# Attention's edges in a four-layer image kernel: a split image load, a pair of queries moved behind a branch, a last chunk ended by products, and norms in text order

## The chip, the cores and the metric

The kernel runs on one core of a Trainium2 chip. The metric is the device time of one execution in microseconds (us). Three runs of the kernel before the change gave 7595.06, 7599.12 and 7599.31 us; the median is 7599.12 us. One further execution was taken with the hardware profiler, and all views shown are of that one. Engines are named as the profile names them: PE is TensorE, DVE is VectorE, ACT is ScalarE, POOL is GpSimd, SP is SyncE, which here only issues transfers.

## The reference

One image of 48 channels and 128 x 128 pixels, float32, passes through four layers with residuals:

```
x = x + attention(group_norm(x))      # layer 0
x = x + sweeps(group_norm(x))         # layer 1
x = x + patch_conv(group_norm(x))     # layer 2
x = x + scan(group_norm(x))           # layer 3
```

`group_norm` has 16 groups of 3 channels and takes mean and variance over a group's whole image. Layer 0 makes queries, keys and values by a 1x1 convolution and a 3x3 depthwise one, divides each query and key by its length, multiplies the scores of all 16384 pixels against all 16384 by a temperature, takes a softmax, sums the values, and applies a 48 x 48 projection. Layer 1 runs four recurrences, one row or column a step, in which a row receives a 5-tap convolution of the row before: down, up, right, left. Layer 2 is a convolution with products of 8x8 Fourier transforms, layer 3 a state-space scan. The change touches layer 0, the way into layer 1, and the loading of the image.

## The kernel before

**Storage.** Two large tiles, `xa` and `xb`, are used again and again. In attention `xa` is called `xq`, `xb` is called `other`. The image is loaded into partitions 0 to 47 of `xa`, in eight transfers on SP's queue (L1549), followed there by the sweep weights. In `xb` the columns 0 to 8191 become the keys `k` (pixels of the first half of the image on partitions 0 to 63, of the second on 64 to 127), the columns above the values `v`. The queries are written over the image in `xa`, on partitions 0 to 63 by VectorE and again on 64 to 127 by a ScalarE copy.

**Statistics and bands.** 32 `bn_stats` (L162) over 512 pixels each, then `group_stats` (L71 to L87): an aggregation, two tiny products that average over a group, a square root on ScalarE, a reciprocal. The convolution runs over eight bands of 16 rows. For a band, VectorE writes the normalised rows (L93), SP copies them to partitions 64 to 111 (L188) and parts of them to the free partitions (L190), and makes twelve small copies for the taps that are left (`rest`, L199). Two `bands` tiles alternate, and the next band is prepared while this one is worked on. A band is worked on in two pairs of 512 pixels: `conv` is the products, `take` squares, sums, takes the root (`nrm`), transposes the values (`pt`), and scales queries and keys by the reciprocal length on VectorE (L263 to L271). TensorE and ScalarE instructions are held to text order by `InOrder`; other engines are ordered by a scheduler.

**The branch.** A register is loaded from `absT`, the size of the temperature, and all engines branch: to `attend` when it is at most 32, which is the case here, else to `attend_shifted`, which subtracts each query's largest score.

**attend.** 32 chunks of 512 queries; in each 64 key tiles `j`, each with four score products (L48, `s`), one exponential of 128 x 1024 on ScalarE (`e`), and four products that add weighted values and weights into `acc`. The sums follow two tiles behind the scores (`BEHIND`). A chunk is ended by `Finish`: ScalarE copies `acc` to `o`, VectorE adds its two halves (`both`, L366), ScalarE copies the upper partitions down (`second`), VectorE adds (L372) and takes the reciprocal of the weights' sums (L375), SP copies the reciprocals to the channels' partitions in three transfers (L378), VectorE multiplies, adds the image, and takes `bn_stats` of the result (L382 to L384), and SP stores the chunk to `x1` (L385). For all chunks but the last these steps lie under the next chunk's products.

**Into layer 1.** POOL clears borders in `xb` and sets a row of ones (`borders`, L610 to L614); `group_stats` again; 32 ScalarE instructions of 8 rows (L623) write the normalised image twice into `xb`; then the sweeps start: each step has an input product (L653), three state products (L678) and a VectorE multiplication by a mask into the next row.

Of the kernel before, what the change touches and what calls it, by code (L numbers as in the profile page):

```python
# [65 lines left out]
def group_stats(nc, pool, psum, const, name="gn_ps"):  # L66


    st, gmat = const["st"], const["gmat"]
    mv = pool.tile([C, 2], F32, name="gn_mv")  # L70
    nc.vector.bn_aggr(mv, st)  # L71
    pm = psum.tile([C, 1], F32, name=name)
    nc.tensor.matmul(pm, lhsT=gmat, rhs=mv[:, 0:1], start=True, stop=True)
    mean = pool.tile([C, 1], F32, name="gn_mean")
    nc.vector.tensor_copy(mean, pm)

    dev = pool.tile([C, 1], F32, name="gn_dev")
    nc.vector.tensor_sub(dev, mv[:, 0:1], mean)
    var = pool.tile([C, 1], F32, name="gn_var")
    nc.vector.scalar_tensor_tensor(var, dev, dev, mv[:, 1:2], ALU.mult, ALU.add)  # L80
    pv = psum.tile([C, 1], F32, name=name)
    nc.tensor.matmul(pv, lhsT=gmat, rhs=var, start=True, stop=True)
    std = pool.tile([C, 1], F32, name="gn_std")
    nc.vector.tensor_scalar_add(std, pv, 1e-5)
    nc.scalar.activation(std, std, AF.Sqrt)
    rstd = pool.tile([C, 1], F32, name="gn_rstd")
# [27 lines left out]
def attention(ctx, tc, xq, other, x1, const, ins):  # L114


    nc = tc.nc
# [11 lines left out]
    nc.sync.dma_start(proj[0:GAP, 0:C], ins["l0_proj"])  # L129
    temp = kv.tile([128, 1], F32, name="temp")  # L130
    nc.sync.dma_start(temp, ins["l0_temp"].to_broadcast([128, 1]))
# [5 lines left out]
    nc.vector.tensor_mul(absT, temp, sgn)  # L137

    with ExitStack() as a:
# [21 lines left out]
        for i in range(NQ):  # L161
            nc.vector.bn_stats(st[:, i, :], xq[0:C, i * CH : (i + 1) * CH])  # L162
        stats = group_stats(nc, wp, ps2, const, name="pss")
# [9 lines left out]
        def band(b):  # L173

            t, e = bands[b % 2], rests[b % 2]
            first = b * R - 1
            lo, hi = max(first, 0), min(first + R + 2, H)
            normalise(  # L180
                nc,
                t[0:C, lo - first : hi - first, 1 : W + 1],
                rows(xq[0:C, lo * W : hi * W]),
                stats,
            )
            if b == NB - 1:
                nc.gpsimd.memset(t[0:C, hi - first : hi - first + 1, :], 0.0)
            nc.sync.dma_start(t[64 : 64 + C, 0 : R + 1], t[0:C, 1 : R + 2])  # L188
            for n in range(2):
                nc.sync.dma_start(  # L190
                    t[64 * n + C : 64 * n + 64, 0:R], t[16 * n : 16 * n + 16, 2 : R + 2]
                )

            two = t[32:C, 2:, :].rearrange("c (k n i) w -> c n k i w", n=2, i=4)
            for i in range(R // 8):
                for n in range(2):
                    for dx in range(3):
                        at = 64 * n + 16 * dx
                        nc.sync.dma_start(e[at : at + 16, i], two[:, n, i, :, dx : dx + W])  # L199
            return t, e  # L200
# [39 lines left out]
        def take(t0, p, pv):  # L240
# [8 lines left out]
            for n in range(2):  # L249
                psss.append(ps2.tile([128, CH], F32, name="pss"))  # L250
                pe.matmul(psss[n], lhsT=blk, rhs=sqs[n], start=True, stop=True)
                nrms.append(sp.tile([128, CH], F32, name="nrm"))
                act.activation(nrms[n], psss[n], AF.Sqrt)
            pt = ps1.tile([128, 4, 2, 64], F32, name="pt")
# [6 lines left out]
            left = []  # L261
            for n in range(2):
                nc.vector.tensor_scalar_max(nrms[n], nrms[n], 1e-12)  # L263
                rn = sp.tile([128, CH], F32, name="rn")
                nc.vector.reciprocal(rn, nrms[n])
                q = slice(t0 + n * CH, t0 + (n + 1) * CH)
                nc.vector.scalar_tensor_tensor(
                    xq[0:64, q], p[n][0:64], sgn[0:64], rn[0:64], ALU.mult, ALU.mult
                )
                left.append(q)  # L270
                nc.vector.tensor_mul(  # L271
                    k[kb : kb + 64, tk + n * CH : tk + (n + 1) * CH], p[n][64:128], rn[64:128]
                )
            nc.vector.tensor_copy(
# [8 lines left out]
        for b in range(NB):  # L283
            nxt = band(b + 1) if b + 1 < NB else None
            for y in range(0, R, 8):
# [4 lines left out]
                for q in left:  # L290
                    act.copy(xq[64:128, q], xq[0:64, q])
# [1455 lines left out]
```

## Time and profile before

| | |
|---|---|
| median of three runs | 7599.12 us |
| the profiled execution | 7597.49 us |
| its span, first to last instruction | 7595.7 us |
| PE busy | 6125.8 us, 81% |
| ACT busy | 4410.3 us, 58% |
| DVE busy | 3378.7 us, 44% |
| POOL busy | 2792.3 us, 37% |
| attention's score and sum products | 252.47 to about 3778 us |
| first product of the sweeps | 3804.74 us |

A line of the timeline has the start and the duration in us, the engine (with q: its queue, where transfers are issued), the line of the kernel, the operation, what is written and read, the shapes, and how many such instructions are merged in the line; in brackets stand the idle time before it and what ended it. Where an order is kept by the helper `InOrder`, the line is L48 for all instructions, so that tiles' names tell them apart. A row of the windows has, for a stretch of time, its length and then the busy time and count of PE, PE's weight loads, DVE, ACT and POOL, then the granted TensorE clock, the mean busy share of the 16 DMA engines, and GB/s. The chain is the work that ended last, followed back from the last instruction.

### The profile page before, as it was taken

What the parts mean: (1) busy time and instruction counts of PE and PEld (TensorE: products, weight loads), DVE (VectorE), ACT (ScalarE), POOL (GpSimd) and SP (SyncE); (2) the same over time, 40 slices, a digit from 0 to 9 for tenths busy, and PEclk for the clock granted to TensorE, in tenths of its full rate; (3) what the DMA queues carried; (4) which work ended last, traced back from release to release, by engine and by line L of the source; (5) the groups of instructions that cost most, each with busy time, mean ns of one, the idle gap of its engine ahead of it and who ended that gap; (6) DMA issues with size and microseconds to landing.
All of it is one profiled execution on the core that took longest, in us unless ns stands there. A gap on an engine that the chain in (4) does not pass through costs nothing.

```text
span 7595.7 us, 203249 instructions
## 1 busy us (share of the span) xinstructions
PE 6125.8 (81%) x93756; PEld 3162.8 (42%) x93756; DVE 3378.7 (44%) x2497; ACT 4410.3 (58%) x4868; POOL 2792.3 (37%) x574
## 2 busy tenths in 40 slices
PE   7999999999999999999988889755545545554555
PEld 3333333333333333333367755334334343343444
DVE  8300000000000000000022234499999999999998
ACT  2566666666666666666625003366666667666665
POOL 0000000000000000000000022299999999999998
PEclk9999999999999999999999999876767767776666
DMA  3000000000000000000000011166556665656775
GB/s 66 8 4 4 4 3 4 4 4 3 4 4 3 4 4 4 3 4 4 4 1 17 1 33 37 46 160 165 158 158 167 156 160 154 164 159 164 177 181 150
DMA packets 182350, 484.85 MB, mean 64 GB/s; under 512 B 35859, under 2 KB 67778, under 8 KB 179506
## 3 DMA queue, kind: packets, MB, share of 16 engines
q1 hardware_dynamic: 175471, 464.69, 24.0%
q8 instruction: 735, 12.04, 0.7%
q10 hardware_dynamic: 6019, 7.09, 0.4%
q14 instruction: 125, 1.02, 0.0%
HBM read 428.03 MB, written 22.02 MB: 59 GB/s over the span
## 4 chain that ended last, share of the span: by engine, by line
PE 58%; DVE 24%; issue 7%; POOL 4%; ACT 2%; DMA 1%; SPq 0%; DVEq 0%; POOLq 0%; ACTq 0%
PE s L48 23%; PE acc L48 23%; DVE h L1504 20%; PE p L678 6%; POOL h L1497 3%; PE y L48 2%; DVE xb L48 1%; DVE xa L48 1%; DMA du<-rep 1%; PE pp L48 1%; PE pc L48 1%; PE po L48 1%; ACT dA L48 1%; DVE y L48 0%; POOL y L901 0%
## 5 line engine op out<-in xcount | busy, mean ns | idle before, releaser
L48 ACT ACTIVATE e<-s,absT 128x1024 f32<-128x1024 f32 x2048 | 2279.2, 1115 | 1197.5 <-PE s L48 1196.7
L1497 POOL TENSOR_TENSOR h<-du,bt 128x3072 f32<-128x3072 f32 (+1 forms) x386 | 2560.0, 6672 | 83.2 <-DMA du<-rep 62.1
L48 PE MATMUL s<-xa,xb 49*64 49x512 f32 x16384 | 2133.9, 589 | 10.6 <-DVE xb L271 10.6
L48 PE MATMUL acc<-e,xb 64*64 64x512 f32 x16384 | 2131.9, 588 | 0.0
L1504 DVE TENSOR_TENSOR_SCAN h<-dA,carry,h 128x1024 f32<-128x1024 f32 x864 | 1939.8, 2329 | 43.3 <-ACT dA L48 27.2
L48 ACT ACTIVATE dA<-dt,a 128x1024 f32<-128x1024 f32 x1152 | 1287.3, 1118 | 867.5 <-DVE h L1504 856.4
L48 PE MATMUL y<-h,cw 128*32 128x48 f32 x49152 | 886.2, 244 | 933.2 <-issue 499.0
L366 DVE TENSOR_TENSOR both<-o 128x512 f32<-128x512 f32 x32 | 22.2, 693 | 3078.6 <-ACT o L48 3078.6
L614 POOL MEMSET xa<- 48x128 f32 x1 | 0.3, 326 | 3523.5 <-PE acc L48 3523.5
L48 PEld LDWEIGHTS y<-h,cw 128*32 128x32 f32 x49152 | 796.5, 138 | 1057.8 <-issue 653.1
L48 PEld LDWEIGHTS s<-xa,xb 49*64 49x64 f32 x16384 | 643.9, 132 | 1129.9 <-issue 587.3
L48 PEld LDWEIGHTS acc<-e,xb 64*64 64x64 f32 x16384 | 643.1, 132 | 1118.9 <-issue 1096.0
L1504 DVE TENSOR_TENSOR_SCAN h<-dA,h 128x1024 f32<-128x1024 f32 x288 | 633.9, 2270 | 44.8 <-ACT dA L48 36.0
L48 PE MATMUL yz<-ev,sel 128*8 128x48 f32 x4096 | 193.5, 260 | 280.0 <-ACT ev L48 274.3
L48 PEld LDWEIGHTS yz<-ev,sel 128*8 128x8 f32 x4096 | 162.7, 106 | 338.3 <-ACT ev L48 305.9
L678 PE MATMUL p<-xb,l_w 112*112 112x129 f32 x1524 | 233.6, 289 | 42.6 <-DVE xb L48 42.5
L678 PE MATMUL p<-xa,l_w 112*112 112x129 f32 x1524 | 232.2, 288 | 41.9 <-DVE xa L48 41.9
L699 POOL TENSOR_TENSOR xb<-xb,xa 48x2048 f32<-48x2048 f32 (+2 forms) x10 | 44.7, 4465 | 559.0 <-DVE xa L48 559.0
L678 PEld LDWEIGHTS p<-xb,l_w 112*112 112x112 f32 x1524 | 181.9, 177 | 94.1 <-DVE xb L48 94.1
L661 ACT COPY xa<-xb 48x128 f32<-48x128 f32 x256 | 107.3, 419 | 194.5 <-issue 136.0
L678 PEld LDWEIGHTS p<-xa,l_w 112*112 112x112 f32 x1524 | 180.6, 176 | 93.3 <-DVE xa L48 93.3
L48 PE MATMUL pc<-wt,xa 128*128 128x288 f32 x768 | 198.8, 416 | 7.4 <-DMA xa<-xa 7.4
(186 smaller groups left out, 3349.7 us busy)
## 6 DMA issues: line engine op xcount, KB each, us to landing
du<-rep SPq DMA_DIRECT2D x768, 256.0 KB
dt<-rep SPq DMA_DIRECT2D x768, 256.0 KB
rep<-dd SPq DMA_DIRECT2D x24, 192.0 KB
yd<-ys ACTq DMA_DIRECT2D x256, 12.0 KB
rest<-xa SPq DMA_DIRECT2D x90, 38.0 KB
band<-band SPq DMA_DIRECT2D x8, 414.4 KB
xa<-in_x_dram SPq DMA_DIRECT2D x8, 384.0 KB
rest<-band SPq DMA_DIRECT2D x96, 32.0 KB
```

Source lines behind the costliest of these rows:

```text
L48: ins = method(*args, **kwargs).ins
L366: nc.vector.tensor_add(self.both, o[:, 0], o[:, 1])
L614: nc.gpsimd.memset(b[64:K, lines, E + W - 1 : E + W], 0.0)
L661: nc.scalar.copy(u[at : at + C, :, y], t[0:C, E + h, E : E + W])
L678: nc.tensor.matmul(p, lhsT=w[0:K, which, i, :], rhs=state[0:K, 2 * i : 2 * i + L], start=False, stop=(i == 2),)
L699: nc.gpsimd.tensor_add(xr, xr, u[0:C, x : x + xr.shape[2], E : E + H].rearrange("c w h -> c h w"),)
L1497: nc.gpsimd.tensor_mul(h[:, p, ks], du.unsqueeze(1).to_broadcast([128, ks.stop - ks.start, LC]), r["bt"][:, ks],)
L1504: nc.vector.tensor_tensor_scan(h[:, p, k, :], dA, h[:, p, k, :], carry[:, i, k : k + 1] if ci else 0.0, ALU.mult, ALU.add,)
```

## The change

The image is loaded into `xb` instead: the first half of the pixels on partitions 0 to 47, the second on 64 to 111, in alternate transfers, with POOL memsets ahead on partitions 32 to 63. `bn_stats` covers both halves in 16 instructions, and a new table `gmat2` averages over groups and halves. The first band is prepared in two parts, of which the first one's small copies are issued on ACT's queue; the loads of `proj` and `temp` move from SP's queue to ACT's. The last pair's norms and products are copied by ScalarE to `late`, and their scaling is put into both branches (`scale`, `again`). Attention's last chunk adds partitions by two products with a 0-1 matrix (`adder`) instead of by copies; its store to `x1` is issued behind the branch. After the branch ScalarE takes a square root of `absT`, which nothing reads. The chunk pool has one buffer instead of two. The borders' memsets go by 16 rows, and the fills are in text order with two smaller ones first. The core of the diff:

```
-        for i in range(NQ):
-            nc.vector.bn_stats(st[:, i, :], xq[0:C, i * CH : (i + 1) * CH])
-        stats = group_stats(nc, wp, ps2, const, name="pss")
+        K2 = 64 + C
+        halves = wp.tile([K2, NQ // 2, 6], F32, name="halves")
+        for i in range(NQ // 2):
+            nc.vector.bn_stats(halves[:, i, :], other[0:K2, i * CH : (i + 1) * CH])
+        mean, rstd = group_stats(nc, wp, ps2, halves, const["gmat2"], name="pss")
+        stats = mean[0:C], rstd[0:C]
...
+            for p0, p1 in [(0, 10), (10, R + 2)] if b == 0 else [(0, R + 2)]:
+                for half, x in enumerate((other[0:C], other[64 : 64 + C])):
+                    lo = max(first + p0, half * H // 2)
+                    hi = min(first + p1, (half + 1) * H // 2)
+                    if lo < hi:
+                        at = half * H // 2
+                        normalise(
+                            nc,
+                            t[0:C, lo - first : hi - first, 1 : W + 1],
+                            rows(x[:, (lo - at) * W : (hi - at) * W]),
+                            stats,
+                        )
...
+                queue = nc.scalar if b == 0 and p0 == 0 else nc.sync
+                for i in range(to.start // 8, to.stop // 8):
+                    for n in range(2):
+                        for dx in range(3):
+                            at = 64 * n + 16 * dx
+                            queue.dma_start(e[at : at + 16, i], two[:, n, i, :, dx : dx + W])
...
+            if t0 == N - 2 * CH:
+                for n in range(2):
+                    act.copy(late[n], p[n])
+                p = late
...
+            def scale():
+                for n in range(2):
+                    nc.vector.tensor_scalar_max(nrms[n], nrms[n], 1e-12)
+                    rn = rnp.tile([128, CH], F32, name="rn")
+                    nc.vector.reciprocal(rn, nrms[n])
...
+            if p is not late:
+                scale()
...
+    end = slice(N - CH, N)
+    nc.sync.dma_start(x1[:, end], xq[0:C, end])
+    nc.scalar.activation(absT, absT, AF.Sqrt)
+
+def adder(nc, pool, ident):
+    add = pool.tile([128, 64 + C], F32, name="add")
+    nc.vector.memset(add, 0.0)
+    for b in (0, 64):
+        nc.vector.tensor_copy(add[b : b + C, 0:C], ident[b : b + C, b : b + C])
+        nc.vector.tensor_copy(
+            add[b + 32 : b + 64, 64:], ident[b + 32 : b + 64, b + C : b + C + 1].to_broadcast([32, C])
+        )
+    return add
...
-    sp = ctx.enter_context(tc.tile_pool(name="l0_b", bufs=2))
+    sp = ctx.enter_context(tc.tile_pool(name="l0_b", bufs=1))
...
+    def end():
+        cols = slice(N - CH, N)
+        xres = sp.tile([C, CH], F32, name="xres")
+        nc.sync.dma_start(xres, ins["x"][:, cols])
+        o = sp.tile([128, 2, CH], F32, name="o")
+        act.copy(o, acc)
+        p = ps_s.tile([128, 2, CH], F32, name="s")[0 : 64 + C, 0]
+        for part in range(2):
+            pe.matmul(p, lhsT=add, rhs=o[:, part], start=(part == 0), stop=(part == 1))
+        rec = sp.tile([64, CH], F32, name="rec")[0:C]
+        nc.vector.reciprocal(rec, p[64 : 64 + C])
+        nc.vector.tensor_mul(rec, p[0:C], rec)
+        nc.vector.tensor_add(xq[0:C, cols], rec, xres)
+        nc.vector.bn_stats(st[:, NQ - 1, :], xq[0:C, cols])
+
+    scale, again = last
+    scale()
+    add = adder(nc, ep2, ident)
...
+            if c == 0 and j == KT // 2:
+                again(act.copy)
...
-    finish = Finish(NQ - 1, acc)
-    finish.divide()
-    finish.result()
+    end()
...
-        nc.gpsimd.memset(b[32:64, lines, inside], 1.0)
+        for r in range(lines.start, lines.stop, 16):
+            some = slice(r, r + 16)
+            nc.gpsimd.memset(b[32:64, some, inside], 1.0)
+            nc.gpsimd.memset(b[0:C, some, E - 1 : E], 0.0)
...
-    RN = 8
-    for r in range(0, H, RN):
+    act = InOrder(tc, nc.scalar)
+    for lo, hi in [(0, 2), (2, 8)] + [(r, r + 8) for r in range(8, H, 8)]:
         for at, x in ((0, E), (64, E - 1)):
-            nc.scalar.activation(
+            act.activation(
...
-        for i in range(0, N, 2048):
-            nc.sync.dma_start(xa[0:C, i : i + 2048], ins["x"][:, i : i + 2048])
+        for i in range(0, N // 2, 2048):
+            nc.gpsimd.memset(xb[32:64, i : i + 2048], 0.0)
+            for half in range(2):
+                at = half * N // 2 + i
+                nc.sync.dma_start(
+                    xb[64 * half : 64 * half + C, i : i + 2048], ins["x"][:, at : at + 2048]
+                )
```

## The prediction

> **What bounds the kernel now.** I read the page first, for which work follows which, then the timeline of the four places that the change touches, then the windows of the first 30 us and the waits of SyncE. The profiled execution took 7597.49 us (span 7595.7, so 1.8 us lie around it); the median of the three runs, 7599.12, stands 1.6 us above it.
>
> ```profile
> PE 58%; DVE 24%; issue 7%; POOL 4%; ACT 2%; DMA 1%; SPq 0%; DVEq 0%; POOLq 0%; ACTq 0%
> ```
>
> The chain that ended last is mostly TensorE: attention's score and sum products, then the row-by-row sweeps, then the scan on VectorE. None of these loops is altered. What the change can win lies in the gaps between stages, where the chain passes from engine to engine. There are three.
>
> *Start.* From the timeline, the windows and SyncE's waits:
>
> ```profile
> 0.74 9.86 SPq L1549 DMA_DIRECT2D xa<-in_x_dram  x8
> 12.35 17.49 DVE L162 BATCH_NORM_STATS2 st<-xa 48x6 f32<-48x512 f32 x29
> 29.87 1.01 DVE L71 BATCH_NORM_AGGREGATE gn_mv<-st 48x2 f32<-48x192 f32 x1
> 33.18 3.92 DVE L93 TENSOR_SCALAR band<-xa,gn_mean,gn_rstd 48x2176 f32<-48x2176 f32 x2
> 35.74 0.64 SPq L188 DMA_DIRECT2D band<-band  x1
> 36.42 3.35 SPq L190 DMA_DIRECT2D band<-band  x2
> 42.46 7.86 PE L48 MATMUL p<-band,wt 128*128 128x512 f32 x12 [10.21 <-DMA band<-band]
> ```
> ```profile
> 8.00:10.00 2.00, 0.00 (x0) 0.00 (x0) 0.00 (x0) 0.00 (x0) 0.00 (x0) 1.00 1.10 396
> 14.00:16.00 2.00, 0.00 (x0) 0.00 (x0) 2.00 (x5) 0.17 (x1) 0.00 (x0) 1.00 1.08 152
> 26.00:28.00 2.00, 0.00 (x0) 0.00 (x0) 2.00 (x5) 0.00 (x0) 0.00 (x0) 1.00 0.89 274
> ```
> ```profile
> SPq L1549 <- DMA ident<-in_c_ident_dram: 4.8, 1, 4.8
> ```
>
> VectorE takes the image's statistics without a pause to 29.84 us; then group norm, the first band, its copies, and the first product at 42.46. The last column of the windows is GB/s: the image alone (48 partitions) moves at about 150 with all DMA engines busy, tables of 128 partitions at 274 to 396. The image ends at about 26 us, so loading and statistics are nearly level.
>
> *Branch.* TensorE ends the convolution's transposes, and starts scores 10.6 us later:
>
> ```profile
> 241.27 0.60 PE L48 MATMUL pt<-ident,vt 128*128 128x128 f32 x4
> 241.47 0.60 ACT L48 ACTIVATE nrm<-pss 128x512 f32<-128x512 f32 x1 [0.26 <-PE pss L48]
> 252.47 5.40 PE L48 MATMUL s<-xa,xb 49*64 49x512 f32 x24 [10.60 <-DVE xb L271]
> ```
>
> The releaser is VectorE's scaling of the last pair of queries and keys. Between these gaps TensorE is never idle: its other waits in 43 to 240 us are none.
>
> *End of attention to the first sweep step:*
>
> ```profile
> 3778.48 1.01 ACT L48 COPY o<-acc 128x1024 f32<-128x1024 f32 x1 [1.40 <-PE acc L48]
> 3779.87 13.91 POOL L610 MEMSET xb<- 32x16512 f32 x1
> 3781.62 3.34 DVE L375 RECIPROCAL rec<-y 32x512 f32<-32x512 f32 x1
> 3784.99 1.78 SPq L378 DMA_DIRECT2D recs<-rec  x3
> 3789.70 0.69 DVE L384 BATCH_NORM_STATS2 st<-xa 48x6 f32<-48x512 f32 x1
> 3792.96 1.01 DVE L71 BATCH_NORM_AGGREGATE gn_mv<-st 48x2 f32<-48x192 f32 x1 [2.58 <-issue]
> 3795.59 1.28 ACT L85 ACT_TABLE_LOAD   x1 [14.72 <-DVE gn_std L84]
> 3797.56 39.24 ACT L623 ACTIVATE xb<-xa,off,gn_rstd 48x1024 f32<-48x1024 f32 x32 [0.47 <-DVE off L619]
> 3804.74 0.74 PE L653 MATMUL p<-xb,l_wi 112*112 112x129 f32 x2 [9.41 <-ACT xb L623]
> ```
>
> Every step here waits for the one above it, the memset excepted.
>
> **The change part by part.**
>
> *Load and statistics.* Half the image goes to partitions 0 to 47, half to 64 to 111, so one statistics instruction covers both: 16 instead of 32 at 0.668 us, 10.7 us less on VectorE. But the image must have landed. It is 8 x 384 KB, 3.15 MB; at about 150 GB/s, 21 us. If the two halves ran side by side it would be 10.5 us. The Trainium skill speaks against that: "SBUF — State Buffer", section "Can I just issue two DMAs to hit both halves?", says that two DMAs at once, one at partition 0 and one at 64, gave only 6% over one, since they serialize on the same engines. By the rule 1.2 us are saved, by the hope 10.5. No row here shows alternate halves. I stand near the rule, since all eight loads stay in one queue, and take 10%, 1.9 us. Against it: the second load now waits for the identity table, as the third does above, and for a POOL memset (32x2048, 1.7 us by 13.91 us for 16512), and behind it in SP's queue wait six loads and the sweep weights. I estimate 1 us, plus 0.3 us for a 50 KB table. The image then ends 0.6 us sooner, at about 25.3; 1 us to land, four statistics of 0.668: 29.0 instead of 29.87, **0.9 us**. Ends: 1.5 us lost if nothing runs faster; 8 us won if halves run side by side, which VectorE then caps, because in the built change all 16 statistics stand behind the weight multiply that waits for both weight loads (now queued later, the first of them behind the first image load). The POOL memsets delay the bands' memsets by 7 us, to about 13.6, with the bands written at 33. Moving two small loads from SP to ACT costs nothing: they are issued while ACT is idle.
>
> *Group norm and first band.* Aggregation over 96 values instead of 192: 0.5 of 1.01. The Sqrt table loads early, because the projection's copy is no longer late: 0.2. **0.7 us.** The first part of the band has 9 rows of 17: 2.53 us (17 rows, 1x2176) becomes 1.3, **1.2 us**. The copies before the first product shrink from 414 and 2 x 130 KB to 52% of that: about 690 KB took 4.6 us, now 2.4; 0.5 is given back to six small copies that go at once on ACT's queue: **1.7 us**. On ACT six issues of 0.64 us, 3.8 us, stand before the first square, 9 us after the first product; covered. On SP, past which they are moved, part two of the band follows; it is wanted 14.8 us after the first product. Two later bands get a normalisation more (some 0.2 us each), within VectorE's idle (22.5 us before L263 over the stage). Whole start: 0.9 + 0.7 + 1.2 + 1.7 = **4.5 us**.
>
> *Branch.* ACT copies the last pair out of PSUM (2 x 0.59, by the row of vt, same shape), and VectorE's scaling moves behind the branch. In the built change the first score waits for the pair before (done at about 240) and for the second of these copies; a wait for the last pair's keys stands at the 57th key tile, 56 x 1.72 = 96 us later, for 10.3 us of VectorE work. ACT's norm ends at 242.07, the copies at 243.3; with 0.15 us, as the old hand-over took, scores start at 243.4 instead of 252.47: **9.0 us**. TensorE's branch itself was issued at 240.8 and took 95 ns, so is no cost. ACT then makes the previous pair's two copies (1.14 us, as before), ready at 244.5; its Exp table waits for the first score tile anyway, some 2.2 us after the start. The last pair's copies stand between Exps: 1.24 us against 0.6 us idle in each of 1.72 us and two tiles of lead (sums follow scores by 2): no stall, 1.2 us if that cover is gone. The x1 store is issued behind the branch, nobody waits for 250 us.
>
> *Attention's last chunk.* Removed: both (0.69), second (0.62), y (0.68), three copies through SP (3784.99 to 3788.20, 3.2 us). Added: two products with the adder, as the norm's two pss products (1.98 us). Reciprocal, multiply, add and statistics stay. 3779.5 + 2.0 + 3.35 + 0.7 + 0.7 + 0.7 with hand-overs is 3787.1 instead of 3790.39: **3.3 us**. The adder's five small VectorE instructions lie in the first chunk, hidden.
>
> *Out of the branch.* The 2.58 us "issue" before aggregation stays: it follows VectorE's own last instruction and no transfer. The table load leaves the chain: ACT does a Sqrt at once after the branch, about 3783 (its copy at 3778.5, a jump of 3.3 us as VectorE's, the load), before aggregation at 3789.7 which waits for it: **1.3 us**.
>
> *Fill.* Before, the first product waited for the sixth fill, 7.2 us after the first began. In text order it needs two of 2 rows (256 elements, about 0.4 us each by 1.15 to 1.24 for 1024): 0.85 us, **6.3 us**. The next product wants two of 6 rows, 1.75 us, under the 2.5 us which the first step takes. Later 8 rows cost 2.4 us of ACT and 10.4 us of steps. POOL's memset of 13.91 us ended at 3793.8, which would now hold the fills (from 3793.0); in eight pieces the first fill waits for the first only, and most are released within the last chunk. If that cover failed, about 1 us.
>
> Sum: 4.5 + 9.0 + 3.3 + 1.3 + 6.3 = **24.4 us**. 7597.5 - 24.4 = 7573.1 for a profiled execution, 7574.7 by the median; I say 7574.5.
>
> **The rivals.** *Halves load side by side.* For: the windows show more than double the rate on 128 partitions with the engines busy either way, so the receiving side limits; staggered engines could use both. Against: the rule. Another 7 us: 7567.
>
> *A gap stays shut.* Scores still start after the scaling (9.0 us gone, 7583.7), or memsets, mask or jump hold the sweeps (10.9 in all gone, 7585.6). For: VectorE still has to do all of it, and was 98% busy before the branch. Against: the waits above.
>
> *Slower: single buffers.* The chunk pool goes from two buffers to one. If the copy of acc, which itself releases the one acc, had to wait for its single buffer, TensorE would stall at 31 boundaries. It ends slower by over 0.2% from (24.4 + 15.2)/31 = 1.3 us each; at 2 us the time is 7637. For: acc already waits there, 16.4 us in 31 times. Against: VectorE idles 93.66 us before both, so the buffer is free long before.
>
> **How the numbers follow.** About what a measurement can tell from no change is 0.2%, 15.2 us, or 7583.9. Main case 0.68 (7570 to 7580), side by side 0.15, gap shut 0.13 (a third still beyond the bound), slower 0.04. Faster 0.68 + 0.15 + 0.05 = 0.88, same 0.08, slower 0.04. The range reaches into the side-by-side and shut cases: 7563 to 7584.
>
> **What would show it.** Right: first statistics aggregation near 29 and first convolution product near 38; scores 1.5 us after the transposes; aggregation 11.3 us after the last sums of attention (14.6 now); the first sweep product under 1 us after the first fill. Wrong: 250 GB/s or more while only the image loads; TensorE waiting for L295 before the first score; waits of TensorE at chunk boundaries.

## The result and the profile after

The changed kernel took 7579.23 us (median of nine runs, 7572.69 to 7580.31). The kernel before took 7600.40 us beside it (median of nine, 7595.06 to 7607.28). The ratio is 0.997, 95% interval 0.996 to 0.998. That is 21.2 us less, where 24.6 were forecast. A second set, on another occasion, gave 7574.90 us (five runs) against 7603.35 (nine): 0.9964, interval 0.9950 to 0.9977, 28.5 us less. The forecast of 7574.5 lies just under both medians of the changed kernel, its gain of 24.6 us between the two gains.

The profiled execution of the changed kernel took 7579.86 us (span 7578.1). First its start, from the timeline: start, duration, engine, line, operation, tiles, shapes, and in brackets the idle time before and what ended it.

```profile
0.73 11.38 SPq L1616 DMA_DIRECT2D xb<-in_x_dram  x8
15.06 2.46 DVE L169 BATCH_NORM_STATS2 halves<-xb 112x6 f32<-112x512 f32 x4
27.01 2.47 DVE L169 BATCH_NORM_STATS2 halves<-xb 112x6 f32<-112x512 f32 x4 [2.11 <-DMA xb<-in_x_dram]
29.52 0.59 DVE L71 BATCH_NORM_AGGREGATE gn_mv<-halves 112x2 f32<-112x96 f32 x1
34.16 0.64 SPq L205 DMA_DIRECT2D band<-band  x1
34.20 5.53 ACTq L217 DMA_DIRECT2D rest<-band  x6
38.97 7.44 PE L48 MATMUL p<-band,wt 128*128 128x512 f32 x11 [7.04 <-DMA band<-band]
```

VectorE no longer works through the statistics: it waits for the image in front of each later group of four (the first waits for the weights' multiply). Aggregation comes at 29.52 instead of 29.87, the first convolution product at 38.97 instead of 42.46. Two rows of the windows (the last three columns are the clock, the DMA engines' busy share and GB/s), and a wait of SyncE:

```profile
6.00:8.00 2.00, 0.00 (x0) 0.00 (x0) 0.47 (x3) 1.28 (x1) 1.94 (x3) 1.00 0.62 131
18.00:20.00 2.00, 0.89 (x5) 0.70 (x4) 2.00 (x4) 1.05 (x2) 0.00 (x0) 1.00 1.02 176
```
```profile
SPq L1616 <- DMA ident<-in_c_ident_dram: 4.6, 1, 4.6
```

While only the image loads it moves at 152 to 188 GB/s (mean of 14 to 24 us: 173; before: 148). But from 4 to 8 us the DMA engines are only two thirds busy, because SyncE waits: the second image load counts its landing on the semaphore that counted the table's, so it is not issued before the table has landed.

The branch:

```profile
238.49 1.07 ACT L48 COPY late<-p 128x512 f32<-128x512 f32 x2
239.66 2.81 PE L48 MATMUL s<-xa,xb 49*64 49x512 f32 x24 [1.26 <-POOL xb L308]
243.45 1.09 PE L48 MATMUL acc<-e,xb 64*64 64x512 f32 x8 [0.99 <-ACT e L48]
```

Scores start at 239.66 instead of 252.47, 1.3 us after the transposes. And what was not forecast: the first 24 score instructions (a float32 product is two of them) take 2.81 us instead of 5.40. Before, the granted clock was 0.50 there, now it is 1.00; the row of before:

```profile
254.00:256.00 2.00, 2.00 (x16) 0.64 (x12) 0.00 (x0) 1.29 (x2) 0.00 (x0) 0.50 0.16 46
```

The groups of the page show that the one buffer costs nothing; these are TensorE's whole waits in attention (last column, us):

```profile
L48 PE MATMUL s<-xa,xb 49*64 49x512 f32 x16384 | 2124.7, 588 | 1.3 <-POOL xb L308 1.3
L48 PE MATMUL acc<-e,xb 64*64 64x512 f32 x16384 | 2124.0, 588 | 1.0 <-ACT e L48 1.0
```

The end of attention and the first steps of the sweeps:

```profile
3763.62 1.01 ACT L48 COPY o<-acc 128x1024 f32<-128x1024 f32 x1 [1.38 <-PE acc L48]
3764.68 1.97 PE L48 MATMUL s<-o,add 128*112 128x512 f32 x4 [1.13 <-ACT o L48]
3766.29 1.28 ACT L336 ACT_TABLE_LOAD   x1 [1.66 <-issue]
3771.52 0.69 DVE L447 BATCH_NORM_STATS2 st<-xa 48x6 f32<-48x512 f32 x1
3774.66 1.01 DVE L71 BATCH_NORM_AGGREGATE gn_mv<-st 48x2 f32<-48x192 f32 x1 [2.46 <-issue]
3778.01 22.27 ACT L48 ACTIVATE xb<-xa,off,gn_rstd 48x256 f32<-48x256 f32 x19 [0.47 <-DVE off L683]
3779.37 0.74 PE L717 MATMUL p<-xb,l_wi 112*112 112x129 f32 x2 [2.31 <-ACT xb L48]
3790.02 1.63 PE L742 MATMUL p<-xb,l_w 112*112 112x129 f32 x6
3792.04 0.92 PE L742 MATMUL p<-xb,l_w 112*112 112x129 f32 x6
```
```profile
3788.00:3790.00 2.00, 2.00 (x9) 1.74 (x8) 0.29 (x1) 1.97 (x2) 0.42 (x2) 0.50 0.00 0
3792.00:3794.00 2.00, 1.81 (x15) 1.60 (x15) 0.29 (x1) 1.96 (x3) 1.47 (x2) 1.00 0.00 0
```

The first product of the sweeps comes at 3779.37 instead of 3804.74, 25.4 us sooner. Then six steps run with a granted clock of 0.50, 2.02 us from one to the next; the seventh is the first at full clock, 1.30 us. Before, only two steps were slow:

```profile
3807.25 1.63 PE L678 MATMUL p<-xb,l_w 112*112 112x129 f32 x6
3809.27 0.92 PE L678 MATMUL p<-xb,l_w 112*112 112x129 f32 x6
```

The lead, read from one trace of each kernel at the same work:

| mark | before | changed | lead |
|---|---|---|---|
| first convolution product | 42.46 | 38.97 | 3.5 |
| first score product | 252.47 | 239.66 | 12.8 |
| last copy of `acc` | 3778.48 | 3763.62 | 14.9 |
| first product of the sweeps | 3804.74 | 3779.37 | 25.4 |
| tenth step of the sweeps | 3818.44 | 3796.01 | 22.4 |
| first `dA` of the scan | 4934.67 | 4910.73 | 23.9 |
| end of the span | 7595.7 | 7578.1 | 17.6 |

From the first `dA` to the end the kernel before took 2661.0 us and the changed one 2667.3. Nothing there was altered. In the fourteen traces of this study that stretch lies between 2658.1 and 2670.9 us, without order by kernel, so one execution says little about an edge of a few us by its whole time. The experiments are therefore read at marks near their edit.

### The profile page after: what moved, and what is told of

It is laid out like the page before. It is cut to its first block, busy times and chain, and to the rows that moved or that the text cites. A ratio compares the mean times of both kernels' runs of the same rounds, so it can differ in the third digit from the quotient of the medians.

```text
span 7578.1 us, 203332 instructions
## 1 busy us (share of the span) xinstructions
PE 6136.3 (81%) x93760; PEld 3145.5 (42%) x93760; DVE 3370.9 (44%) x2487; ACT 4409.3 (58%) x4872; POOL 2802.6 (37%) x606
```

## The experiments

Runs 1 to 10 are one profiled execution each; of runs 11 and 12 five executions each were timed. The kernel before, run beside them, took 7596.79 us (runs 1 to 4), 7604.62 (5 to 8), 7599.49 (9 and 10) and 7603.35 (11 and 12).

**Theory.** The edges were won as forecast; what the sum lacked is TensorE's clock, which adds 2 us at the branch and takes up to 3 at the sweeps; and the load won less than its rate allows because its second transfer waits. **Rivals:** ScalarE or the fills limit those places; alternating halves bring no rate; the memset is off the path.

**1. The sweeps' start, filled.**

```
+    warm(11)     # products identity x l1_w, 128x512, into a PSUM tile that nothing reads
     mean, rstd = group_stats(nc, pool, ps1, const["st"], const["gmat"], pe=pe)
+    warm(4)
```

> Fifteen products that nothing reads (identity by sweep weights, 128x512) fill TensorE's idle time between attention's end and the first product of the sweeps: eleven before the statistics' products, four behind them. Theory (a clock that halves after idling takes the missing gain): the changed kernel's granted clock is 0.50 from 3774 to 3791 us and its first six steps take 2.0 us each instead of 1.3; with the fill the clock stays at 1.00, state products take 0.92 us from the first step or the second, the first product stays 1.4 us behind the first fill, and the tenth step comes about 4 us sooner after the first fill (12.7 us of cold steps become about 8.5). Rival (the first steps wait for fills by ScalarE, not for the clock): the steps keep 2.0 us for the first 12 us whatever the clock shows, no gain. Whole time about 7576 against 7579.9 by the theory, 7580 by the rival; one look can't tell these, the trace does.

Measured: 7583.0 us. The fill was too large: a float32 product of 128x512 is two instructions of 0.43 us at full clock (0.85 at half), so fifteen are thirty; moreover the first waited for VectorE to let go of the PSUM bank. The norm's products were nearly 8 us late. Counted from the first fill by ScalarE, though, the tenth step came after 14.57 us instead of 18.00, with 1.30 us a step from the first on and clock 1.00:

```profile
3787.79 0.82 PE L754 MATMUL p<-xb,l_w 112*112 112x129 f32 x6
```

ScalarE's fills hence don't force 2 us a step; the clock does: the rival falls. The experiment confirms the mechanism, not a gain.

**2. The scores' start, filled in the kernel before.**

```
+        for n in range(18):
+            if n % 9 == 0:
+                pw = ps2.tile([128, CH], F32, name="pss")
+            pe.matmul(pw, lhsT=ident, rhs=wt.rearrange("c t o -> c (t o)")[:, 0:CH], start=True, stop=True)
```

> The kernel before, with eighteen products that nothing reads (identity by weights, 128x512) in TensorE's 10.6 us of idle time before the first score; nothing else is changed, so the scores still start at about 252.5 us. Theory (2 us of the changed kernel's gain at the branch is a TensorE that had no time to fall to half clock): the first 24 score products take 2.8 us instead of 5.4, the granted clock is 1.00 at 252 us, the first exponential starts about 1.8 us and the first sum product 2.0 us sooner than the before's 255.99 and 257.61 us, and the end of the last sums is 2 us sooner (3776.4 instead of 3778.48). Rival (the 2 us come from ScalarE: its copies and its table load stand elsewhere in the changed kernel): scores 2.8 us, but the first sum still near 257.6, no gain.

Measured: 7611.85 us. The same double count: 36 instructions, 15.6 us, so that the scores started at 257.94, 5.5 us late. From there on the timeline and windows read as the theory has them:

```profile
257.94 2.81 PE L48 MATMUL s<-xa,xb 49*64 49x512 f32 x24
261.73 1.09 PE L48 MATMUL acc<-e,xb 64*64 64x512 f32 x8 [0.99 <-ACT e L48]
```
```profile
258.00:260.00 2.00, 2.00 (x20) 0.87 (x24) 0.00 (x0) 0.73 (x1) 0.00 (x0) 1.00 0.33 100
```

From the first score to the last copy of `acc` it is 3523.99 us, in the kernel before 3526.01, in the changed one 3523.96. So 2.0 us of the changed kernel's gain are the clock alone: in the kernel before the 10.6 us of idle time ahead of the scores left it at 0.50 (windows from 246 to 258 us), in the changed one the 1.3 us did not. The rival, ScalarE's order, falls: it was that of before here, and the 2.0 us came all the same.

**3. The identity table last.**

```
-        ("ident", [128, 128]),
         ("gmat", [C, C]),
...
+        ("ident", [128, 128]),
```

> The changed kernel with the identity table moved from the first to the last of the five tables on ScalarE's queue, so that the second image load waits for a table of 9 KB instead of one of 64 KB. Theory (the halves gain 15 to 20% of rate, and the 4.6 us wait of SyncE for the table, with DMA engines 0.62 to 0.69 busy from 4 to 8 us, took some 1.5 us of it back): SyncE's wait falls to about 2 us, the DMA engines are at 0.9 or more from 4 us on, the last statistics and the aggregation come 1.5 us sooner (28.0 instead of 29.52), the first convolution product at 37.5 instead of 38.97. Rival (the load's end is set by something later, such as the weights' transfers or the third wait of 3.2 us): aggregation stays within 0.4 us of 29.5.

Measured: 7580.19 us; aggregation at 30.57, first convolution product at 40.02, no gain. SyncE now waited 4.5 us for `gmat`, 9 KB, as it had 4.6 for `ident`, 64 KB:

```profile
SPq L1616 <- DMA gmat<-in_c_gmat_dram: 4.5, 1, 4.5
```

The size of the table is not the cause: the first image load is issued at the same time, and a small transfer from the other queue lands no sooner. My reading of the wait was wrong by that much.

**4. The same, and the sweep weights loaded later.** The two loads of `l1_w` and `l1_wi` move from behind the image to behind the first band's copies, held there by `InOrder`.

> As the run with the identity table last, and the two loads of sweep weights (516 and 172 KB) are issued behind the first band's copies instead of behind the image. Theory (the image's landing sets the start, VectorE only follows): these weights no longer share the DMA engines with the last image loads; by the 2 us rows about 175 KB of them moved before the image's end, 1.0 us at 170 GB/s. Aggregation near 27.0 us, first convolution product near 36.5. Rival (VectorE caps it: 16 statistics of 0.62 us can't start before the weights' multiply at 14.2 us): aggregation not before 15.1 + 9.9 = 25.0 us, so the rival would show as statistics without a pause and an end near 25; and if neither holds, 28.0 as without this edit.

Measured: 7573.48 us, but aggregation at 30.49 against 30.57 in run 3: nothing from the weights. They stood behind the image in the same queue, and what they took of its rate is less than the start varies by itself. The image's last packet was moved from 26.33 to 27.23 us, and VectorE was released at 27.99. The whole time is 6.7 us under run 3 because the scan took 2660.2 instead of 2667.3 us.

**5. The tables through GpSimd's queue.**

```
-        nc.scalar.dma_start(const[name], ins[f"c_{name}"])
...
+        pool = InOrder(tc, nc.gpsimd)
         for i in range(0, N // 2, 2048):
-            nc.gpsimd.memset(xb[32:64, i : i + 2048], 0.0)
+            pool.memset(xb[32:64, i : i + 2048], 0.0)
...
+        for name in ("ident", "gmat", "gmat2", "blk", "eye2"):
+            pool.dma_start(const[name], ins[f"c_{name}"])
```

> The changed kernel with the five tables loaded through GpSimd's queue, behind its memsets of xb; so no image load shares its turn with a table, and the second load needs only the first memset. The two runs before showed that not the size of the table counts: SyncE waited 4.5 to 4.8 us for one of 9 KB as for one of 64 KB, because a table's landing waits behind the first image load. Theory (that wait leaves the DMA engines idle by 0.3 to 0.4 from 4 to 8 us, 1.5 us, and it ate the gain of the halves): the engines are 0.9 busy or more from 2 us on, aggregation comes 1.5 us sooner (28.0 instead of 29.5 to 29.9), the first convolution product near 37.5. Rival (another order of the same bytes ends at the same time): aggregation within 0.4 us of 29.7.

Measured: 7571.60 us; aggregation at 27.65, first convolution product at 37.17. From the windows and the timeline of this run:

```profile
6.00:8.00 2.00, 0.00 (x0) 0.00 (x0) 0.24 (x2) 0.00 (x0) 2.00 (x3) 1.00 1.09 193
18.00:20.00 2.00, 1.33 (x7) 0.84 (x6) 1.02 (x2) 0.58 (x1) 0.00 (x0) 1.00 0.99 202
```
```profile
27.65 0.59 DVE L71 BATCH_NORM_AGGREGATE gn_mv<-halves 112x2 f32<-112x96 f32 x1
```

The engines stay busy from 4 us on, and the image's last packet ends at 24.25 us instead of 25.87. The mean of 194 GB/s from 14 to 24 us is not the image's alone: the five tables (0.2 MB) moved from 14.7 to 20.8 us and the sweep weights from 21.9, and the image's own packets make 145. In seven traces whose load is that of the changed kernel, aggregation came at 28.91 to 30.48 us, mean 29.9; in the two that load as before, at 29.63 and 29.87. So the load is worth 2.2 us here against the kernel before, 1.3 in run 11, which loads in the same way (28.61), and nothing by the mean of the seven: the wait had eaten it.

**6. One half after the other.** The order of the eight loads: four to partitions 64 to 111, then four to 0 to 47.

```
-            for half in range(2):
+        sp = InOrder(tc, nc.sync)
+        for half in (1, 0):
+            for i in range(0, N // 2, 2048):
...
-                nc.sync.dma_start(
+                sp.dma_start(
```

> The changed kernel with the eight image loads in another order: all four of the second half (partitions 64 to 111), then all four of the first. Theory (it is the alternation between two ranges of partitions that lifts the rate from a mean of 147 GB/s in the kernel before, 12 to 24 us, to 166 to 172 in four runs, 14 to 26 us): the windows with only the image fall back to about 147, the image ends some 2.5 us later, aggregation near 32. Rival (the rate is the same on either range, and what changed is how the queues mix): 165 to 170 GB/s, aggregation within 0.5 us of 29.7, with the first statistics later since they need both halves.

Measured: 7582.89 us; 131 to 176 GB/s from 14 to 28 us, mean 146.6, which is the rate of the kernel before; aggregation at 32.46. A row of its windows:

```profile
20.00:22.00 2.00, 0.10 (x1) 0.00 (x0) 0.00 (x0) 1.66 (x2) 0.00 (x0) 1.00 0.98 147
```

Alternation is what lifts the rate: from 14 to 24 us the nine traces with alternating loads and tables on ScalarE's queue moved 164 to 191 GB/s (mean 174), the three without alternation 144 to 148, so 19% more by the means. How fast the image would move without the wait and without other transfers beside it, no run shows. The Trainium skill, "SBUF — State Buffer", section "Can I just issue two DMAs to hit both halves?", has 6% for two transfers at once, at partitions 0 and 64; for loads in turn on one queue the measurement decides.

**7. The fills as before.**

```
-    act = InOrder(tc, nc.scalar)
-    for lo, hi in [(0, 2), (2, 8)] + [(r, r + 8) for r in range(8, H, 8)]:
+    act = nc.scalar
+    for lo, hi in [(r, r + 8) for r in range(0, H, 8)]:
```

> The changed kernel with the fills of the sweeps' rows as before: 8 rows each from the first, in the scheduler's order instead of the text's. Theory (text order is worth 5.8 to 6.3 us): the first sweep product comes 7.2 us after the first fill instead of 1.36, so at about 3785.2 if the first fill stays at 3778. The tenth step's distance from the first fill grows by 5.8 us, plus or minus multiples of 0.72 us for each step more or less that runs at half clock (2, 4 and 6 such steps have been seen). Rival (rows come late again under text order, so that the win is given back within the first rows): the tenth step is no later than in the changed kernel, 18.0 us after the first fill.

Measured: 7565.95 us, the lowest of runs 1 to 10. From its timeline:

```profile
3777.00 29.03 ACT L687 ACTIVATE xb<-xa,off,gn_rstd 48x1024 f32<-48x1024 f32 x23 [0.47 <-DVE off L683]
3779.65 0.74 PE L717 MATMUL p<-xb,l_wi 112*112 112x129 f32 x2 [3.60 <-ACT xb L687]
```

The first product follows the first fill by 2.65 us, neither 1.36 nor 7.2. The scheduler put the first row's two fills in front by itself; they are only larger, which costs 1.3 us. With the memset in pieces, text order and the smaller first fills together are worth no more than that. That the run is fast has other grounds: two cold steps instead of six, and a scan of 2658.1 us.

**8. The sweeps' start filled with the right number.**

```
+        w = ps_a.tile([128, 2, CH], F32, name="acc")[0 : 64 + C, 0]     # in end()
+        for _ in range(9):
+            pe.matmul(w, lhsT=add, rhs=o[:, 0], start=True, stop=True)
...
+    for _ in range(2):                                                  # behind group_stats
+        pe.matmul(pw, lhsT=const["ident"], rhs=flat[:, 0:CH], start=True, stop=True)
```

> The changed kernel with nine products in attention's end, behind the adder's (adder by o, each two passes of 0.43 us, 7.7 us in all), and two (1.7 us) behind the group norm's second product; nothing reads them. They fit into the idle time of TensorE, which the first try overfilled (a float32 product of 128x512 counts twice). Theory (half clock costs the sweeps' start 0.72 us a step): clock 1.00 from 3764 to the sweeps, first fill still 14.4 us after the copy of acc, first product 1.0 us after it, steps of 1.3 us from the first on, tenth step 14.3 us after the first fill instead of 18.0 (the overfilled try had 14.6). Rival (the idle gap of 2.3 us before the first product is enough to halve the clock again): steps of 2.0 us for 4 to 12 us as before.

Measured: 7582.69 us. First fill 14.2 us after the copy of `acc`, so nothing was delayed; tenth step 14.12 us after it instead of 18.00. The timeline shows what comes next when the clock does not limit:

```profile
3779.82 0.82 PE L753 MATMUL p<-xb,l_w 112*112 112x129 f32 x6
3781.55 0.47 PE L728 MATMUL p<-xb,l_wi 112*112 112x129 f32 x2 [0.90 <-ACT xb L48]
3783.14 0.91 PE L753 MATMUL p<-xb,l_w 112*112 112x129 f32 x6 [0.24 <-DVE xb L48]
```

The second step waits 0.9 us for the fills of 6 rows. That the whole time shows no gain: the clock fell to 0.50 once more at 4113 us, in the middle of the sweeps, for 14 us, and the scan took 2669.6 us.

**9. The pause in the middle, filled.** Between the upward and the rightward sweep TensorE waits 1.36 us for ScalarE's turn. In six of the twelve traces without a fill there, the clock then fell for 3 to 14 us.

```
+            for _ in range(5):     # behind the load of x1
+                pe.matmul(pw[0:K, 0:L], lhsT=w[0:K, 0, 0, :], rhs=state[0:K, 0:L], start=True, stop=True)
             nxt = begin(up)
```

> As the run with nine and two products that nothing reads, and five more (112x129, two passes each, 1.1 us in all) in the middle of the sweeps, in the 1.36 us in which TensorE waits between the upward and the rightward sweep. In five of ten traces the clock fell to 0.50 there, for 8 to 14 us. Theory (a pause of that length is enough when it falls badly, and it is the rest of the sweeps' spread): no window of the sweeps below 0.98 clock; tenth step 14.1 us after the first fill as before, and 663 us from the tenth step to the first pc product, the least that was seen (663.0 in five traces, 665.1 to 665.6 in three, 668.0 in two). Rival (the clock falls in the sweeps by itself, with or without the pause): again 665 or 668 with a dip near 4112 us.

Measured: 7580.48 us, and the experiment failed as built: the five products read rows of `xb`, which the load of x1 overwrites, and stood behind it in the text. TensorE waited 5.6 us for the load, and the clock fell to 0.50. It says nothing of the pause itself. The start of the sweeps was at full clock again (tenth step 14.56 us after the first fill).

**10. The memset in one piece.**

```
-        for r in range(lines.start, lines.stop, 16):
-            some = slice(r, r + 16)
+        for some in [lines]:
```

> The changed kernel with the borders' memset of ones in one piece of 128 rows (13.9 us on GpSimd) as before, but the fills still in text order with the small ones first. The run with the old fills and the memsets in pieces lost only 1.3 us: its scheduler put the first row's fills first by itself. Theory (it is the pieces of the memset that brought the rest of the 5.8 us, 4.5: in the kernel before the first row's fill stood sixth because it waited for the whole memset): ScalarE's first fill now waits for GpSimd until about 3783 us instead of 3778, the first product follows 1.4 us later, 5 us later than in the changed kernel (20.7 instead of 15.75 us after the copy of acc starts). Rival (the order is what counts, and the memset is off the path): first fill 14.4 us after the copy of acc as in the changed kernel, no loss, at most the 1 us that the prediction gave a failed cover.

Measured: 7577.16 us. From its timeline:

```profile
3770.99 13.92 POOL L675 MEMSET xb<- 32x16512 f32 x1
3784.94 3.31 ACT L48 ACTIVATE xb<-xa,off,gn_rstd 48x256 f32<-48x256 f32 x4 [5.93 <-POOL xb L675]
```

The first fill waits 5.9 us for GpSimd and comes 19.9 us after the copy of `acc` (begun at 3765.06) instead of 14.4: 5.5 us lost. The first product then follows by 1.36 us as in the changed kernel. So text order without the pieces closes the distance from first fill to first product, but the fill comes late; the pieces without text order (run 7) keep all but 1.3 us. The memset is on the path: the rival falls, and the theory holds for the changed kernel. For the kernel before it is not shown: there the memset began 1.39 us after the copy of `acc` and ended at 3793.78, 3.8 us ahead of the first fill. Here it began 5.93 us after the copy, behind the branch, which is 4.5 of the 5.5 us by that difference.

**11 and 12. A version with the tables and the fills, and the changed kernel again, on the same chip.** Run 11 takes the edits of runs 5 and 8, moves the five products of run 9 ahead of the load of x1, and adds five products of 128x512 behind the first group norm.

```
+        warm(5)                 # behind group_stats in attention()
...
         if n + 1 == up:
+            for _ in range(5):
+                pe.matmul(pw[0:K, 0:L], lhsT=w[0:K, 0, 0, :], rhs=state[0:K, 0:L], start=True, stop=True)
```

> The changed kernel with what the runs pointed to: tables through GpSimd's queue; five unread products (10 passes) between the first group norm and the first convolution product; nine and two before the sweeps; five in the pause in the middle of the sweeps, now issued ahead of the load of x1, for which they wrongly waited 5.6 us in the run with three fills. By the traces: start 1.8 us (37.2 instead of 39.0 for the first convolution product), first twelve convolution products at full clock 2.3 us (5.3 instead of 7.4 to 7.9), first steps of the sweeps 2.9 us (0.72 by the mean of 4 cold steps), middle 1.6 us (half the traces lose 2.2 to 5). Theory (half clock is most of what the edges still cost): 8.6 us less than the changed kernel, 7570.6 where that takes 7579.2. Rival (the scan, whose length from the first dA to the end was 2654 to 2671 us in eleven traces, hides it): no difference from the changed kernel.

> The changed kernel again, unaltered, beside the version with fills on the same chip. Theory: 7579.2 as in its nine runs, 0.28% under the kernel before, and about 8.6 us over the version with fills. In its trace the start should be as in the other kernels with its load (first convolution product between 38.4 and 39.4), the sweeps cold for 2, 4 or 6 steps, and the scan anywhere in 2654 to 2671 us. Rival (the nine runs were a lucky chip): 7585 or more, or less than 0.2% under the kernel before.

Measured: 7569.40 us (7565.02 to 7572.43) for run 11, ratio to the kernel before 0.9957, interval 0.9943 to 0.9970; 7574.90 us (7571.95 to 7579.66) for run 12. The version with fills is 5.5 us faster than the changed kernel by the medians, where 8.6 were expected; the two ranges overlap by 0.5 us. In the traces its lead at the first `dA` is 8.6 us over the first trace of the changed kernel and 9.8 over run 12's (4902.14, 4910.73, 4911.92), and the scans of 2661.1 and 2661.7 us are alike. (The range of 2654 to 2671 us in the two texts above is a slip: the lowest of the traces is 2658.1.) From its timeline:

```profile
38.18 5.39 PE L48 MATMUL p<-band,wt 128*128 128x512 f32 x12 [0.57 <-DMA band<-band]
3773.62 1.99 PE L48 MATMUL warm<-l_w,ident 128*128 128x512 f32 x4
3776.28 0.82 PE L759 MATMUL p<-xb,l_w 112*112 112x129 f32 x6
4107.50 1.26 PE L48 MATMUL warm<-xb,l_w 112*112 112x129 f32 x10
4109.03 0.45 PE L48 MATMUL p<-xa,l_wi 112*112 112x129 f32 x2 [0.27 <-ACT xa L48]
```

The first twelve convolution instructions take 5.39 us instead of 7.87, and neither at the start of the sweeps nor in their middle does a window show less than full clock. For the middle that is one trace, where half of the others had no dip either: it agrees with the pause as the cause and doesn't show it by itself. Aggregation came at 28.61, not at 27.65 as in run 5; that much the start varies.

## Why the prediction was right

By the steps of its sum, each between the same two marks in the traces of before and of the changed kernel:

| step | forecast | measured |
|---|---|---|
| load and statistics | 0.9 | 0.35 (29.87 to 29.52); nothing by the mean of seven traces |
| group norm | 0.7 | 0.16 |
| first part of the band | 1.2 | 1.07 |
| its copies | 1.7 | 1.91 |
| branch | 9.0 | 9.32 |
| clock at the branch | none | 2.05 |
| last chunk | 3.3 | 3.32 |
| table load out of the chain | 1.3 | 1.37 |
| fills | 6.3 | 5.82 |
| sum at the first sweep product | 24.4 | 25.37 |

That the sum agrees so well is in part luck: the load, the group norm, the band's first part and the fills fell 1.70 us short, and the clock, which was not in the sum, gave 2.05.

The branch, the last chunk and the table load stand as worked out, and the rival in which a gap stays shut did not come: nothing took the place of VectorE's scaling or of the jump. The rival of single buffers did not come either; the groups show no wait at a chunk's boundary. Of the marks named for the main case, the product near 38 came at 38.97, scores 1.3 us after the transposes (1.5 said), aggregation 11.1 us after the last sums (11.3 said), the first sweep product 1.36 us after the first fill (under 1 said: the two fills of 2 rows took 0.60 us each, not about 0.4, and the hand-over 0.15).

*Mis-sized: the load.* The step took 10% more rate and charged 1.3 us for waits. The rate rose by 17% in this trace (148 to 173 GB/s), and the wait cost nearly all of it: 4.6 us for a table, with a third of the DMA engines' time lost from 4 to 8 us (runs 3, 5, 6). The image's last packet ended at 25.87 us instead of 26.27. The place of the wait was right, its price was not, and the table's size, by which it was priced, does not matter. The rival in which the halves load side by side was right that the rate can rise by more than 10%; twice the rate was not seen in any run.

*Mis-sized: group norm.* Aggregation was 0.42 us shorter and the square root's table was early, as said. But the table for averaging over both halves makes the two tiny products 112 wide, 0.53 us each instead of 0.32, which was not counted: 0.42 given back.

*Right in size, mis-sized in its parts: the fills.* The prediction gave 6.3 us to text order and smaller fills, and about 1 us to the memset if its cover failed. Undone alone, neither costs what it was given. Without text order (run 7) the loss is 1.3 us. Without the pieces (run 10) it is 5.5 us, ahead of the first fill, because there the long memset starts behind the branch, 5.93 us after the copy of `acc` and not 1.39 as before; started as before it would cost about 1 us, as the prediction had it (an estimate: 5.5 less the difference of 4.5). No run undid both, so how the 5.82 us divide between order and pieces stays open.

*Missing: the clock.* The prediction timed moved products at the duration they had, and did not ask what an idle gap does to the products behind it. A gap that was closed gave 2.05 us more than its length. Then the early sweeps took 2.9 us back in the profiled execution, by six slow steps instead of two. That last is no fixed cost of the change: with the sweeps entered as in the changed kernel it was 6, 6, 4, 4, 4 and two and a part slow steps (the changed kernel, runs 4, 3, 5, 6, 12), 2 in runs 7 and 10, and in the kernel before's own way in 2 and 4 (before, run 2).

The end lies about the 24.4 us of the sum: 17.6 in one pair of traces, where the unaltered scan took 6.3 us longer, 21.2 and 28.5 in two sets of runs. The scan alone varies by 12.7 us over the traces; what else moves the medians is not shown.

## What to carry to other kernels

Closing a gap before TensorE is worth its length and also what the idle clock cost the products behind it; so read the granted clock in the windows on both sides of each gap, and where a gap can't be closed, products that nothing reads may fill it, counted by instructions in the trace (two for each float32 product here) and placed so that they wait for nothing. A small table's transfer, issued here beside a large one on another queue, landed with the large one, so what waited for the small one waited for both. A rate is read from windows in which nothing else moves. Read a few us at marks beside the edit: a long unaltered stage can vary by more than the edit is worth.

## What was not expected of the hardware

- TensorE at half clock: steps of the sweeps 2.02 us instead of 1.30. Entering the sweeps after idling, steps at full clock began 4.5 to 12.7 us after the first product, although the steps were alike and TensorE was busy for nearly all of their time at half clock (2.00 of 2.00 us in the row above). In all fourteen traces the changes of the granted clock lie on a grid of 3.41 us, within 0.04 us (in the changed kernel 3771.32, 3791.80 and 4450.58). The Trainium skill, "TensorE: Matmul & The Clock Gate", section "Part 1: The HAM clock gate (the "warmup" mystery)", states a free-running window of about 3.4 us, of which one busy one brings full clock and one idle one takes it. The grid agrees with the window. That one busy window is enough doesn't always hold here: in run 10 the clock rose after one window that the profile has as wholly busy, in the changed kernel after three.
- A pause of 1.36 us between two sweeps was followed by half clock for 3 to 14 us in six of twelve traces, and not in the other six. No window is idle throughout it. The pause lies differently in the grid: in the 3.41 us ahead of the six falls TensorE was busy for 1.50 to 1.89 us, in the least busy window at the pause in the other six for 1.90 to 2.10. The closest two, runs 8 (the clock fell) and 10 (it did not):

```profile
4109.81:4113.22 3.41, 1.89 (x15) 1.51 (x14) 0.59 (x2) 1.77 (x5) 0.00 (x0) 1.00 0.00 0
4118.11:4121.52 3.41, 1.90 (x15) 1.73 (x16) 0.39 (x2) 1.66 (x4) 0.00 (x0) 1.00 0.11 24
```

  That agrees with a limit of busy time in a window, and does not prove one: the ranges nearly touch, and at attention's end, under products of 128x512, the clock stayed full after windows with 1.57 and 1.78 us (runs 10 and 12).
- The image on two partition ranges in turn moved at 164 to 191 GB/s (14 to 24 us, nine traces), on one range or on one after the other at 144 to 148 (three traces).
- A table of 9 KB was waited for 4.5 us beside an image load of 384 KB on another queue.
